# The dilation's first counts and first fixed point in turns with layer 0's last ending

## The chip, the cores and the metric

The kernel runs on one core of one Trainium2 chip. The metric is the device time of one execution in microseconds (us). The engines are named as the profile names them: PE (TensorE; PEld are its weight loads), DVE (VectorE), ACT (ScalarE), POOL (GpSimd), SP (SyncE, which here only issues DMAs). Each engine executes its own queue in order; engines wait for each other through semaphores. [...]

## What is computed

A graph of 1024 nodes with 128 features in each of 16 batches goes through four layers, each added to the running `x` and normed. Two of them matter here, cut to their core:

```python
# layer 0: attention over the adjacency, gate, then x + y, layernorm -> x1
h = x @ W_w.T + W_b
e = einsum('bjl,bkl->bjk', h @ A, h); e = e + swapaxes(e, 1, 2)
att = softmax(where(adj > 0, e, -9e15), axis=1) * adj
h_prime = relu(einsum('bij,bjk->bik', att, h))
coeff = sigmoid(concat([x, h_prime]) @ gate_w.T + gate_b)
y = coeff * x + (1 - coeff) * h_prime

# layer 1: first a sequential dilation of each adjacency, node by node
def step(carry, n):
    row = carry[n]
    num = sum(row)
    sf = where(num > 10, (num + 1) // 2, 1)
    rm = row & (cumsum(row) % sf == 0)      # which neighbours are removed
    keep = ~where(valid, rm, False)
    carry[n] = row & keep;  carry[:, n] = carry[:, n] & keep
# then three graph convolutions over x1 and the dilated adjacency
```

Layers 2 and 3 (a gated attention and a graph convolution) follow and are not touched.

## The kernel before

The batches are b = 0 to 15, NT = 8 tiles of 128 nodes each. The adjacencies of all batches stay in SBUF as 8-bit tiles `Y[b]` (`carry` in the profile), half of them on the left side of SBUF and half on the right.

**Layer 0** (L886 to L1033) runs three streams in rounds (`in_rounds`, L815; a stream yields the number of rounds it pauses). `before(b)` (L923) loads the rows of the adjacency (`an`), turns them to 8 bits, checks their symmetry and prepares the operands `xT`, `G`, `hn`. `attention(b)` (L968) computes scores in PSUM (`wide_matmul`, L724), takes minimum and mask on VectorE (L984), the exponential on ScalarE (L986), and weighs into `acc` (L974). `after(b)` (L999) ends a batch: `hpT` from `acc` (L1002), the gate by small matmuls (L775, L780) and a tanh (L1008), the mix on VectorE (L1014, L1016, L1017), the norm (`normed`, L787: statistics L794 and L796, power on GpSimd L745, `ln_nb` L799, eight activations on ScalarE L801), and the store of `x1_d` (L1020). While batch b is weighed, batch b - 1 ends and batch b + 1 begins. For batch 15 there is no next batch: L1033 runs `after(15)` by itself.

**The dilation** (L1043 to L1202) takes 16 steps: for each tile k of 128 nodes, two groups g of GB = 8 batches. `prepare` (L1057) counts the neighbours for four batches at a time: `uY` (L1072), 32 matmuls into `s0` (L1078), ranks `sk` (L1080), totals `l1` (L1081), `past` (L1084). `fixed_point` (L1089) finds the removals inside the tile in six evaluations, each a comparison `mid` on VectorE (L1106), eight small matmuls `pd` (L1109) and `ti` (L1113), and derives the bounds `negc`, `posc`, `wid` (L1116 to L1139). `removal` (L1142) applies them to one batch: matmuls `s` (L1151, L1153), two activations `q` (L1154), `keep` (L1157), the row update (L1158), the products `pc` (L1161 to L1165) and the write-back (L1166). In the loop (L1198) the fixed point of step i takes turns with the eight removals of step i - 1, which also prepare a later step. The first four `prepare` groups stand ahead of this loop (L1183), and the first round of the loop has the fixed point of step 0 alone. Between them are a flag (L1187, L1188) and `dinv` (L1190 to L1196).

**Layer 1** (L1267 on) starts with batches 8 to 15, whose adjacency needs no load. `first` (L1401) takes the degree product (L1290), copies it (`row`, L1406), sends it through a small DMA (`d`, L1408), and from there come `nodeg`, the reciprocal and the store of `rdeg` (L1409 to L1413). `split` makes `hi` (L1281) and `lo` (L1282) for the adjacency product (L1315); `widened` (L1302, L1304) casts the adjacency. `Step` (L1324) loads its small weights (`Wr`, `Wx`, `b`, `gcol`, `becol`; L703, L693, L698), and `take_norm` (L1341) begins with their sum `ws` (L1345).

**What sets the order.** The functions record instructions in the order of their yields. A scheduler then fixes each engine's queue, so an instruction may stand elsewhere than the source suggests. Pools place tiles in SBUF and PSUM as stacks, from the left or from the right side; a tile waits for the last readers and writers of tiles that lay in the same place before (`reuse_waits="tile"`: tile by tile).

Of the kernel before, what the change touches and what calls it, by code (L numbers as in the profile page):

```python
# [22 lines left out]
P = 128  # L23
# [616 lines left out]
def fast_kernel(ctx: ExitStack, tc: tile.TileContext, t: dict, out: bass.AP, flag: bass.AP):  # L640
# [245 lines left out]
    with ExitStack() as ph:  # L886

        early = ph.enter_context(tc.tile_pool(name="l0_early", bufs=1, reuse_waits="tile"))
        wts = ph.enter_context(tc.tile_pool(name="l0_w", bufs=1, reuse_waits="tile"))
        ps_w = ph.enter_context(tc.tile_pool(name="l0_pw", bufs=2, space=PSUM, reuse_waits="tile"))  # L890
        ps_a = ph.enter_context(tc.tile_pool(name="l0_pa", bufs=1, space=PSUM, reuse_waits="tile"))
        ps_h = ph.enter_context(tc.tile_pool(name="l0_ph", bufs=2, space=PSUM, reuse_waits="tile"))

        with tc.tile_pool(name="l0_raw", bufs=1) as raw:
            W0 = matrix(raw, t["L0_gnn_W_w"], "l0W")
            W0T = transposed(wts, ps_h, W0, "l0WT", "h")
            As0 = symmetric(raw, ps_h, matrix(raw, t["L0_gnn_A"], "l0A"), "l0As", "h")
            AW = raw.tile([P, P], F32, name="l0AW")
            p = ps_h.tile([P, P], F32, name="wtr", tag="h")
            nc.tensor.matmul(p, As0, W0, start=True, stop=True)  # L900
            nc.vector.tensor_copy(AW, p)
            M0 = wts.tile([P, P], F32, name="l0M")
            p = ps_h.tile([P, P], F32, name="wtr", tag="h")
            nc.tensor.matmul(p, W0, AW, start=True, stop=True)
            nc.vector.tensor_copy(M0, p)
            nu = wts.tile([P, 1], F32, name="l0nu")
            p = ps_h.tile([P, 1], F32, name="wtr", tag="h")
            nc.tensor.matmul(p, AW, column(raw, t["L0_gnn_W_b"], "l0b"), start=True, stop=True)
            nc.vector.tensor_scalar(nu, p, -1.0, None, op0=OP.mult)
        work = ph.enter_context(tc.tile_pool(name="l0_work", bufs=1, reuse_waits="tile"))  # L910
        small = ph.enter_context(tc.tile_pool(name="l0_small", bufs=2, reuse_waits="tile"))
        b0 = row_bcast(wts, t["L0_gnn_W_b"], P, "l0brow")
        gw = wts.tile([P, 2, 32], F32, name="l0gw")
        nc.vector.memset(gw, 0.0)
        with nc.allow_non_contiguous_dma(reason="a vector of 256"):
            nc.sync.dma_start(gw[:, :, 0], t["L0_gnn_gate_w"].rearrange("o (h d) -> d (o h)", d=P))
        gb = row_bcast(wts, t["L0_gnn_gate_b"], 1, "l0gb")
        gbh = wts.tile([P, 1], F32, name="l0gbh")
        nc.vector.tensor_scalar(gbh, gb, 0.5, None, op0=OP.mult)
        nbig = wts.tile([P, 1], F32, name="l0nbig")  # L920
        nc.vector.memset(nbig, BIG)

        def before(s, b):  # L923

            s.xn = work.tile([P, NT, P], F32, name="xn", bufs=3)
            nc.sync.dma_start(s.xn, nat(t["x"][b]))
            yield 1
            for it in range(NT):
                c = b * NT + it
                an = early.tile([P, N], F32, name="an", bufs=3)  # L930
                nc.sync.dma_start(an, t["adj"][b][it * P:(it + 1) * P, :])
                nc.scalar.activation(Y[b][:, it, :], an, AF.Copy, accum_out=deg[:, c:c + 1], saturate=False)  # L932

                chk = early.tile([P, N], FP8, name="chk")
                done = (it + 1) * P
                if done < N:
                    nc.vector.scalar_tensor_tensor(chk[:, done:], an[:, done:], 0.0, an[:, done:], op0=OP.is_gt,
                                                   op1=OP.not_equal, accum_out=other[:, b, it:it + 1], saturate=False)
                for h in range(it // 4 + 1):
                    js = range(4 * h, min(4 * h + 4, it + 1))  # L940
                    k = slice(js[0] * P, (js[-1] + 1) * P)
                    pt = ps_h.tile([P, 512], F32, name="pt", tag="h")
                    for i, jt in enumerate(js):
                        nc.tensor.matmul(pt[:, i * P:(i + 1) * P], Y[b][:, jt, it * P:done], identb, start=True, stop=True)
                    nc.vector.scalar_tensor_tensor(chk[:, k], pt[:, :k.stop - k.start], 0.0, an[:, k], op0=OP.is_gt,
                                                   op1=OP.not_equal, accum_out=other[:, b, 7 + it + 4 * h:8 + it + 4 * h],
                                                   saturate=False)
                if it == 2:
                    s.xT = work.tile([P, N], F32, name="xT", bufs=2)
                    for p, c, _ in turned(ps_h, s.xn):  # L950
                        nc.scalar.copy(s.xT[:, c], p)
                elif it == 4:
                    s.G = work.tile([P, N], F32, name="G", bufs=2)
                    for p, c in products(ps_h, (M0, s.xT)):
                        nc.scalar.activation(s.G[:, c], p, AF.Identity, scale=-1.0, bias=nu)
                    pz = gates(ps_h, early.tile([P, N], FP8, name="chk").bitcast(F32), (gw[:, 0, :], s.xT))
                    s.gx = small.tile([P, NT], F32, name="gx")
                    nc.vector.tensor_copy(s.gx.rearrange("p (q t) -> p q t", t=2), pz[:, :, :, 0])
                elif it == 5:
                    s.hn = work.tile([P, N], F32, name="hn")  # L960
                    for p, c, blocks in halves(ps_h):
                        for i, k in enumerate(blocks):
                            nc.tensor.matmul(p[:, i * P:(i + 1) * P], s.xT[:, k * P:(k + 1) * P], W0T, start=True, stop=True)
                        nc.vector.tensor_add(tiles3(s.hn[:, c]), tiles3(p), b0[:, None, :].to_broadcast([P, 4, P]))
                yield 2
            nc.gpsimd.dma_start(adj8_d[b], Y[b].bitcast(F32))

        def attention(s, b):  # L968
            s.acc = ps_a.tile([P, N], F32, name="acc")

            def weigh(jt, hs, em):
                for h in range(H2):
                    c = slice(h * 512, (h + 1) * 512)
                    nc.tensor.matmul(s.acc[:, c], hs, em[:, c], start=(jt == 0), stop=(jt == NT - 1))  # L974

            for jt in range(NT):
                js = slice(jt * P, (jt + 1) * P)
                c = b * NT + jt
                mn = mx0[:, c:c + 1]
                msk = work.tile([P, N], BF16, name="msk", bufs=2)  # L980
                nc.scalar.activation(msk, Y[b][:, jt, :], AF.Identity, scale=-BIG, bias=nbig)  # L981
                e = wide_matmul(ps_w, s.G[:, js], s.xT)
                em = work.tile([P, N], F32, name="em", bufs=2)
                nc.vector.tensor_tensor_reduce(em, e, msk, 1.0, 3.0e38, op0=OP.add, op1=OP.min, accum_out=mn)  # L984
                sm = small.tile([P, 1], F32, name="sm")
                nc.scalar.activation(em, em, AF.Exp, scale=-1.0, bias=mn, accum_out=sm)  # L986
                rs = small.tile([P, 1], F32, name="rs")
                nc.vector.reciprocal(rs, sm)
                hs = small.tile([P, P], F32, name="hs")
                nc.vector.tensor_scalar(hs, s.hn[:, js], rs, None, op0=OP.mult)  # L990
                yield
                if jt:
                    weigh(*late)
                late = jt, hs, em
                yield
            weigh(*late)
            yield

        def after(s, b):  # L999

            hpT = work.tile([P, N], F32, name="hpT")
            nc.scalar.activation(hpT, s.acc, AF.Relu)  # L1002
            yield 3
            pz = gates(ps_h, work.tile([P, NT, P], F32, name="r").rearrange("p t d -> p (t d)")[:, :N // 4], (gw[:, 1, :], hpT))
# [10 lines left out]
            for p, c, k in turned(ps_h, hpT):  # L1015
                nc.vector.tensor_mul(r[:, k, :], tiles3(p), half_rows(co[:, k]))  # L1016
# [8 lines left out]
        for b in range(B):  # L1025
            streams = []
            if b < B - 1:
                streams.append(before(state[b + 1], b + 1))
# [4 lines left out]
        in_rounds([after(state[B - 1], B - 1)])  # L1033

# [803 lines left out]
```

## Time and profile before

| | us |
|---|---|
| median of three runs | 2781.0 |
| lowest, highest | 2775.41, 2783.75 |
| profiled execution: time | 2779.18 |
| profiled execution: span of the instructions | 2777.5 |
| last weighing of layer 0 ends, about | 629.2 |
| layer 0's last activations L801 | 640.92 to 644.1 |
| store of batch 15's rows, from issue | 644.41, 3.9 to landing |
| first fixed point, first `mid` to the last one's end | 651.81 to 664.0 |
| first `q` of the removals | 666.77 |
| last write-back of the dilation, L1166 | 1017.09 to 1018.2 |

The profile records one execution. Its page gives the busy time of each engine over the span and in 40 slices (of 69.4 us here). Its trace answers questions about a stretch of time: a timeline of instructions (start, length, engine, line, operation, output from inputs; in brackets the engine's idle time just before and the instruction that ended it), the chain of waits (followed back from the end of the stretch, at each step to what released it; "issue" is time in which nothing is shown that the engine waited for), and the busy time of each engine in chosen windows, with the granted TensorE clock as a share of full speed. Runs of like instructions are merged (x8). Tile names come without their numbers: `l` is `l1`, `s` in L1078 is `s0`, `x_d` is `x1_d`, `carry` is `Y`.

### The profile page before, as it was taken

How to read it: one execution, taken by the hardware profiler on the slowest of the kernel's cores; microseconds unless marked ns; L12 is line 12 of the kernel's file. 1: busy time of each engine (PE TensorE's matmuls, PEld its weight loads, DVE VectorE, ACT ScalarE, POOL GpSimd, SP SyncE). 2: the span in 40 equal slices, each digit the busy share in tenths (PEclk: the TensorE clock that was granted, in tenths of full speed). 3: DMA queues.
4: the chain of work that ended last, by engine and by line, in shares of the span. 5: the costliest groups of instructions: out<-in, count | busy, mean ns of one | idle time of the engine just before them, and what ended most of it. 6: DMA issues, size and time to landing. Idle time of an engine off the chain costs nothing.

```text
span 2777.5 us, 41717 instructions
## 1 busy us (share of the span) xinstructions
PE 2586.3 (93%) x14808; PEld 1670.4 (60%) x14808; DVE 2131.3 (77%) x5905; ACT 1991.0 (72%) x3316; POOL 334.0 (12%) x287
## 2 busy tenths in 40 slices
PE   7999999995899879998999998999999999999985
PEld 3545444443666658877788894455555555555554
DVE  5888777876999967776788775777778777777865
ACT  6888888974888776666655445877777777777754
POOL 0000000030000002211122141011111111111100
PEclk9999999997999989999999998999999999999998
DMA  5555545520000052233467572111111111121000
GB/s 186 164 162 172 177 161 166 175 89 12 2 2 2 2 219 92 97 117 123 155 235 249 174 267 84 60 62 61 61 61 61 61 61 61 66 68 72 27 20 25
DMA packets 120810, 285.37 MB, mean 103 GB/s; under 512 B 12304, under 2 KB 65424, under 8 KB 113424
## 3 DMA queue, kind: packets, MB, share of 16 engines
q1 hardware_dynamic: 101280, 203.33, 22.3%
q0 software_dynamic: 19312, 79.28, 7.4%
q8 instruction: 119, 1.95, 0.3%
q14 instruction: 99, 0.81, 0.1%
HBM read 202.72 MB, written 79.82 MB: 102 GB/s over the span
## 4 chain that ended last, share of the span: by engine, by line
PE 40%; DVE 19%; ACT 9%; issue 9%; POOL 4%; DMA 3%; POOLq 0%; DVEq 0%; ACTq 0%; SPq 0%
PE pmm L724 6%; PE ph L1605 6%; PE acc L1315 5%; PE acc L1660 5%; PE ph L766 3%; PE ph L759 3%; ACT xn L801 3%; PE acc L974 2%; PE ph L1441 2%; POOL rn L745 2%; DVE em L1673 2%; DVE mid L1106 2%; PE ph L1592 2%; DVE ln_st L794 1%; PE s L1153 1%
## 5 line engine op out<-in xcount | busy, mean ns | idle before, releaser
L745 POOL TENSOR_TENSOR ln_rstd<-ln_rstd,mhalf 128x8 f32<-128x8 f32 (+1 forms) x68 | 121.6, 1788 | 1361.7 <-DVE ln_rstd L742 938.0
L724 PE MATMUL pmm<-xT,G 128*128 128x512 f32 x512 | 261.8, 604 | 0.0
L974 PE MATMUL acc<-em,hs 128*128 128x512 f32 x512 | 260.1, 607 | 1.3 <-DVE hs L990 1.1
L1315 PE MATMUL acc<-a,lo 128*128 128x512 f32 x768 | 240.0, 397 | 17.9 <-DVE lo L1282 17.9
L1660 PE MATMUL acc<-em,hs 128*128 128x512 f32 x512 | 248.6, 601 | 8.1 <-DVE hs L1684 7.8
L724 PE MATMUL pmm<-G,hT 128*128 128x512 f32 x512 | 245.0, 593 | 0.0
L1315 PE MATMUL acc<-a,hi 128*128 128x512 f32 x768 | 240.6, 398 | 3.0 <-ACT hi L1281 2.8
L801 ACT ACTIVATE xn<-xn,ln_nb,ln_rstd 128x128 f32<-128x128 f32 x512 | 205.0, 485 | 48.7 <-DVE ln_nb L799 48.7
L1668 ACT ACTIVATE msk<-A,nbig 128x1024 bf16<-128x1024 fp8e4 x128 | 147.1, 1150 | 73.7 <-DVE mx L1673 48.8
L986 ACT ACTIVATE em<-em,mx 128x1024 f32<-128x1024 f32 x128 | 146.8, 1147 | 59.6 <-DVE mx L984 59.2
L1315 PEld LDWEIGHTS acc<-a,lo 128*128 128x128 f32 x768 | 144.0, 190 | 54.6 <-DVE lo L1282 25.0
L984 DVE CUSTOM_DVE_ANT_0 em<-pmm,msk 128x1024 f32<-128x1024 f32 x128 | 156.3, 1221 | 23.2 <-PE pmm L724 22.4
L1673 DVE CUSTOM_DVE_ANT_0 em<-pmm,msk 128x1024 f32<-128x1024 f32 x128 | 156.3, 1221 | 11.6 <-PE pmm L724 11.3
L1315 PEld LDWEIGHTS acc<-a,hi 128*128 128x128 f32 x768 | 143.4, 190 | 33.1 <-ACT hi L1281 3.7
L1166 ACT ACTIVATE carry<-pc,negone 128x1024 fp8e4<-128x1024 f32 x128 | 141.0, 1115 | 24.4 <-PE pc L1165 19.9
L1605 PE MATMUL ph<-A,zhi 128*128 128x512 f32 x512 | 151.8, 438 | 1.5 <-ACT zhi L1595 1.3
L932 ACT ACTIVATE carry<-an 128x1024 fp8e4<-128x1024 f32 x128 | 134.7, 1052 | 25.9 <-DMA an<-in_adj 25.3
L1677 ACT ACTIVATE em<-em,nmx 128x1024 f32<-128x1024 f32 x128 | 146.2, 1142 | 8.1 <-DVE nmx L1675 7.8
L1660 PEld LDWEIGHTS acc<-em,hs 128*128 128x128 f32 x512 | 90.8, 191 | 92.7 <-issue 69.9
L981 ACT ACTIVATE msk<-carry,l0nbig 128x1024 bf16<-128x1024 fp8e4 x128 | 145.9, 1140 | 0.0
L1304 ACT CAST a<-carry 128x1024 fp32r<-128x1024 fp8e4 x96 | 99.5, 1050 | 50.4 <-PE acc L1315 50.3
L1304 ACT CAST a<-A 128x1024 fp32r<-128x1024 fp8e4 x96 | 99.2, 1050 | 50.3 <-PE acc L1315 50.3
(319 smaller groups left out, 6236.5 us busy)
## 6 DMA issues: line engine op xcount, KB each, us to landing
an<-in_adj SPq DMA_DIRECT2D x128, 512.0 KB, 3.7
adj_d<-carry POOLq DMA_DIRECT2D x16, 1024.0 KB, 4.2
A<-dil_d SPq DMA_DIRECT2D x16, 1024.0 KB, 5.5
rdeg<-rdeg_d SPq DMA_DIRECT2D x32, 512.0 KB, 3.8
A<-adj_d SPq DMA_DIRECT2D x16, 1024.0 KB, 4.8
ag_d<-ag POOLq DMA_DIRECT2D x24, 512.0 KB, 5.2
ag<-ag_d SPq DMA_DIRECT2D x24, 512.0 KB, 5.4
xn<-in_x SPq DMA_DIRECT2D x16, 512.0 KB, 4.3
```

The lines of the kernel that those rows point to most:

```text
L724: nc.tensor.matmul(p[:, h * 512:(h + 1) * 512], lhsT, rhs[:, h * 512:(h + 1) * 512], start=True, stop=True)
L745: nc.gpsimd.tensor_tensor(r, r, mhalf[:, :n], op=OP.pow)
L801: nc.scalar.activation(r[:, k.start + i, :], r[:, k.start + i, :], AF.Identity, scale=rstd[:, i:i + 1], bias=nb[:, i:i + 1])
L974: nc.tensor.matmul(s.acc[:, c], hs, em[:, c], start=(jt == 0), stop=(jt == NT - 1))
L984: nc.vector.tensor_tensor_reduce(em, e, msk, 1.0, 3.0e38, op0=OP.add, op1=OP.min, accum_out=mn)
L986: nc.scalar.activation(em, em, AF.Exp, scale=-1.0, bias=mn, accum_out=sm)
L1304: nc.scalar.copy(a, A[:, 2 * i:2 * i + 2, c])
L1315: nc.tensor.matmul(acc, part[:, jt, :], pieces[h * NT // 2 + i][:, j, :], start=(jt == 0 and p == 0), stop=(jt == NT - 1 and p == 1))
L1605: nc.tensor.matmul(p, part[:, jt, :], A[:, jt, c], start=(jt == 0 and i == 0), stop=(jt == NT - 1 and i == 1))
L1660: nc.tensor.matmul(s.acc[:, c], hs, ex[:, c], start=(jt == 0), stop=(jt == NT - 1))
L1668: nc.scalar.activation(msk, s.A8[:, jt, :], AF.Identity, scale=BIG, bias=nbig, accum_out=zs)
L1673: nc.vector.tensor_tensor_reduce(em, e, msk, 1.0, 0.0, op0=OP.add, op1=OP.max, accum_out=mx)
```

## The change

Layer 0's pools are no longer closed at its end as one. Two stacks of contexts take them: `scores` holds the adjacency's rows (`early`) and the scores' PSUM (`ps_w`), both now on the right side; `ending` holds the rest, on the left. `scores` is closed after the last round of layer 0, and the dilation's pools (SBUF and PSUM, except `ps_c`) are opened on the right side, where those lay. A new stream chains the four `prepare` groups and the fixed point of step 0, and runs in rounds with `after(15)`. Then `ending` is closed, `ps_c` is opened on the left, and the loop starts at step 1. The dilation's pool `small` is renamed `tiny`, since `after` still uses layer 0's `small`. The body of layer 0 is moved out of its `with` block unchanged.

```diff
+    ending, scores = ExitStack(), ExitStack()
+
+    early = scores.enter_context(tc.tile_pool(name="l0_early", bufs=1, side="right", reuse_waits="tile"))
+    wts = ending.enter_context(tc.tile_pool(name="l0_w", bufs=1, reuse_waits="tile"))
+    ps_w = scores.enter_context(tc.tile_pool(name="l0_pw", bufs=2, space=PSUM, side="right", reuse_waits="tile"))
+    ps_a = ending.enter_context(tc.tile_pool(name="l0_pa", bufs=1, space=PSUM, reuse_waits="tile"))
+    ps_h = ending.enter_context(tc.tile_pool(name="l0_ph", bufs=2, space=PSUM, reuse_waits="tile"))
...
+    work = ending.enter_context(tc.tile_pool(name="l0_work", bufs=1, reuse_waits="tile"))
+    small = ending.enter_context(tc.tile_pool(name="l0_small", bufs=2, reuse_waits="tile"))
...
-        in_rounds([after(state[B - 1], B - 1)])
...
+        in_rounds(streams)
+    scores.close()
+
     with ExitStack() as ph:
...
-        sb = ph.enter_context(tc.tile_pool(name="dl_sb", bufs=2, reuse_waits="tile"))
-        small = ph.enter_context(tc.tile_pool(name="dl_small", bufs=3, reuse_waits="tile"))
-        ps_b = ph.enter_context(tc.tile_pool(name="dl_pb", bufs=1, space=PSUM, reuse_waits="tile"))
-        ps_d = ph.enter_context(tc.tile_pool(name="dl_pd", bufs=1, space=PSUM, reuse_waits="tile"))
-        ps_s = ph.enter_context(tc.tile_pool(name="dl_ps", bufs=2, space=PSUM, reuse_waits="tile"))
-        ps_c = ph.enter_context(tc.tile_pool(name="dl_pc", bufs=2, space=PSUM, reuse_waits="tile"))
+        sb = ph.enter_context(tc.tile_pool(name="dl_sb", bufs=2, side="right", reuse_waits="tile"))
+        tiny = ph.enter_context(tc.tile_pool(name="dl_small", bufs=3, side="right", reuse_waits="tile"))
+        ps_b = ph.enter_context(tc.tile_pool(name="dl_pb", bufs=1, space=PSUM, side="right", reuse_waits="tile"))
+        ps_d = ph.enter_context(tc.tile_pool(name="dl_pd", bufs=1, space=PSUM, side="right", reuse_waits="tile"))
+        ps_s = ph.enter_context(tc.tile_pool(name="dl_ps", bufs=2, space=PSUM, side="right", reuse_waits="tile"))
...
-        for s in steps[:G2]:
-            for _ in prepare(*s):
-                pass
+        in_rounds([chain(*(prepare(*s) for s in steps[:G2]), fixed_point(*steps[0])), after(state[B - 1], B - 1)])
+        ending.close()
+        ps_c = ph.enter_context(tc.tile_pool(name="dl_pc", bufs=2, space=PSUM, reuse_waits="tile"))
...
-        for i in range(len(steps) + 1):
+        for i in range(1, len(steps) + 1):
             streams = [fixed_point(*steps[i])] if i < len(steps) else []
-            if i:
-                streams.append(removals(steps[i - 1], steps[i - 1 + G2] if i - 1 + G2 < len(steps) else None))
+            streams.append(removals(steps[i - 1], steps[i - 1 + G2] if i - 1 + G2 < len(steps) else None))
             take_turns(streams)
```

## The prediction, made before the result was known

> **What bounds the kernel now.** I read the page's totals first, then the chain of waits from 600 to 700 us, then the engines' timeline there and at the start of layer 1. The totals:
>
> ```profile
> span 2777.5 us, 41717 instructions
> PE 2586.3 (93%) x14808; PEld 1670.4 (60%) x14808; DVE 2131.3 (77%) x5905; ACT 1991.0 (72%) x3316; POOL 334.0 (12%) x287
> ```
>
> TensorE is busy 93% of the span, but slice 10 of 40 (625 to 694 us) has it at half, and this is where the change acts. The chain of waits there (start, length, what):
>
> ```profile
> 627.27 1.97 PE acc L974 x4
> 629.26 1.03 ACT hpT L1002
> ...
> 639.03 1.66 POOL ln_rstd L745
> 640.69 3.71 issue
> 644.41 3.86 DMA x_d<-xn
> 648.53 0.20 DVE uY L1072
> 648.85 1.32 PE s L1078 x32
> ...
> 662.84 1.24 DVE mid L1106
> 664.12 0.37 PE pd L1109 x8
> 664.50 1.20 PE s L1153 x4
> 665.70 1.08 PE s L1151 x4
> 666.78 0.69 ACT q L1154
> ```
>
> The last weighing ends at 629.2. Then one thread runs alone: batch 15's gate and norm, the store of its rows, the dilation's first counts, six evaluations of the first fixed point. Only at 666.78 does the first removal begin. The timeline (start, length, engine, then in brackets the idle time before and who ended it) says why the counts came so late:
>
> ```profile
> 640.92 3.19 ACT L801 ACTIVATE xn<-xn,ln_nb,ln_rstd 128x128 f32<-128x128 f32 x8 [8.47 <-DVE ln_nb L799]
> 648.37 0.16 DVE L1081 SCALAR_TENSOR_TENSOR l<-s,off 128x4 f32<-128x4 f32 x1 [6.47 <-DMA x_d<-xn]
> 1026.73 0.27 DVE L1409 TENSOR_REDUCE nodeg<-d 8x1 f32<-8x128 f16 x1 [8.72 <-DMA d<-row]
> 1029.24 1.22 PE L1315 MATMUL acc<-a,lo 128*128 128x512 f32 x2 [5.56 <-DVE lo L1282]
> ```
>
> VectorE's first `l1` stood 6.47 us for a store: its small buffer lies where batch 15's `xn` lay. The last two rows are layer 1's start, which the change touches too. The stage tables (length, busy times, granted clock) close the reading:
>
> ```profile
> 629.30:648.50 19.20, 1.99 (x18) 1.28 (x19) 7.73 (x30) 4.86 (x11) 2.58 (x2) 0.68 0.09 27
> 648.50:664.00 15.50, 5.83 (x136) 5.17 (x135) 12.58 (x37) 0.00 (x0) 0.00 (x0) 0.50 0.02 6
> ```
>
> No engine is full in the first stretch; in the second VectorE is busy 12.58 of 15.5 us, TensorE 5.83.
>
> **The change part by part.** No arithmetic goes; it is order and place. I lined up both programs' instructions: up to VectorE's last reduction of the scores (624.10) they differ by two `uY` (0.49 us), placed at 601 us where VectorE idles 0.76 us: nothing. After the dilation's second removal step the orders are equal up to layer 1's start.
>
> *The walk.* I take VectorE's new order, instruction by instruction, with the lengths of before, starting a wait where its producer ends.
> - The first `sk` (0.61) now stands ahead of the last reciprocal, and needs counts that end at 626.55. The last weighing starts 0.6 us later than at 627.27 and ends at 629.85; `hpT` ends at 630.9.
> - TensorE's second group of counts follows that weighing: 629.65 to 630.85. Its `sk` ends at 631.55. From there to the first `mid` it takes 1.0 us (650.80 to 651.81 before): `mid` at 632.6.
> - Before, from first to last `mid` (651.81 to 663.98) it took 12.2 us with the last counts between. Now batch 15's ending stands between: VectorE instructions of 0.24 (gates), 1.14, 2 x 0.65, 1.2, 1.55 (eight statistics), 0.58, 0.2, together 6.2 us. If all of it fell into the waits for `pd` the fixed point would end at 644.8, if none, at 651.0. Following the queue (of each 2.1 us evaluation VectorE works 1.4), 4.1 us stay on the path, since the wide ones (1.14, 1.2) are longer than any gap: 632.6 + 12.2 + 4.1 = 648.9. Before it was 663.98: **15.1 us earlier**.
> - New waits. `ln_nb` stands behind the last `mid` and waits for GpSimd's power: 2.0 us from `ln_rstd` on, as 638.71 to 640.72 before. Queued behind it are `negc`, `posc` and the second fixed point's first `mid`: about 1.1 us of stall. ScalarE has the eight `xn` (3.19) ahead of the first `q`. So 649.0 + 2.0 + 0.2 + 3.2 = 654.4 for the first `q`, against 666.77: **12.4 us earlier**. The second fixed point is 13.5 us ahead; the removals hold the step, so I take 12.4.
>
> *Batch 15's store* lands later, at about 654.4 + 0.3 + 3.9 = 658.6 instead of 648.3. GpSimd's next work is a store at 977.55; layer 1 reads these rows eighth, beyond 1100 us: covered by hundreds of us. But SP's queue meets it. Layer 1's left pools now lie on layer 0's memory, not the dilation's, so its small weights load during the dilation; `b` waits for this store, and behind it stand `gcol`, `becol`, the second `Wr` and `Wx` (rows of 0.45 to 0.69 between issues: the last at 661.3). The scheduler moved the addition that reads them, L1345, from layer 1 into VectorE's queue in the first removal step, with five removals queued behind it. By my walk VectorE gets there at 665.4. A load of this kind landed after 2.1 us (least) to 9.1 (most, among 3 MB of others): 663.4 to 670.4. With SP's queue otherwise empty I take 2.1 to 4.4 and a cost of 0; upper end 5 us.
>
> *dinv and the flags* (L1187 to L1196): moved a few us, 0.8 us of VectorE, with its copy in the stall between the first two counts (628 to 631): 0.
>
> *Layer 1's start.* The degree product's accumulator no longer lies on the removals' last bank, and stands ahead of the last removal's products. The four `row` copies move ahead of two casts of 1 us (18.09 to 20.08 after 1000 before): the path row, store, `d`, `lo` starts 1.9 us earlier. The first loads of `n`, issued at 1015.10 behind VectorE's last `keep`, now follow the loads at 1005.9, so `d<-row` meets less traffic: 5.0 us before, 2.0 in the median of its kind. Lower end 0, upper 1.9 + 3.0 = 4.9; I take **3.0**, as `lo` also needs `hi`, which ends at 1022.4 either way.
>
> [...] The first removals run at a granted clock of 0.5: four matmuls of 128x512 took 1.20 and 1.08 us, later 0.71. [...]
>
> Sum: 12.4 + 3.0 = 15.4. The profiled execution took 2779.2 (span 2777.5 and 1.7 around it), which makes 2763.8; the median of the three runs shown, 2781.0, is 1.8 above it, so **2765.6**. Measured times spread 2775 to 2784, so 0.3%, 8.3 us, is about what this kernel's measurement can tell from no change.
>
> **The rivals.**
> - *The lead is partly given back in the first removal step* (chance 0.2). Three `mid` of the second fixed point now stand ahead of the first `keep`, and products come in bunches ahead of ScalarE's write-backs. A step of before took about 22.1 us (16 steps from 664 to 1018) and needs 19.44 of VectorE in its first 22, so an order that leaves VectorE waiting is not caught up. If 5 us go here and layer 1's start gives 1: 12.4 - 5 + 1 = 8.4, 2772.6. For it: the new order was made on modelled costs. Against it: the same instructions, and later steps regain nothing but lose nothing.
> - *More than I count* (0.2): the clock stays up (2.6) and layer 1's start gives its 4.9: 19.9, 2761.1. Against it is the row above.
> - *The order hides it all* (0.04): within 3 us of before, 2779. VectorE was idle 11.5 of 19.2 us, and no other engine fills that gap, which speaks against it.
> - *Slower than before* (0.03), at L1345: VectorE stops until `Wx` lands. The price is landing minus 665.4. Up to 665.4 it costs nothing, at 670.4 five us; it undoes the gain only from 681 on, and to lose 0.3% it must be 689, a landing 28 us after issue. Nothing of the kind is in the trace, whose slowest such load took 9.1.
> - The likeliest, as summed: 0.53.
>
> The change does move what it says: the new VectorE order has the counts and all six evaluations among batch 15's instructions.
>
> **How the numbers follow.** The likeliest case holds 2761 to 2770 with the spread of a median. The given-back case and the large case lie on both sides, at 2772.6 and 2761.1, and their own spread takes the range to 2756 and 2776. Below 2772.7 lie the likeliest, the large case and about half of the given-back one: faster 0.85; same 0.12; slower 0.03.
>
> **What would show it.** Right: no wait of `l1` for the store; last `mid` of the first fixed point near 649; first `q` near 654.4, directly after ScalarE's eight `xn`; the dilation's last write-back 12 to 13 us earlier than 1018; layer 1's `row` right after it; granted clock near 0.5 at the first removals. Wrong: first `q` after 658 (more of the ending on the path than 4.1 us); a wait at L1345; a removal step of more than 24 us; a layer 1 start that begins earlier and reaches its first `lo` product no sooner.

## The result, and the profile after

Ten runs of the changed kernel have a median of 2767.23 us (2762.59 to 2776.23); the kernel before, on the same chip, 2781.04. The ratio is 0.995, with a 95% interval of 0.9936 to 0.9964: about 13.8 us less, 10 to 18 by the interval. The profiled execution took 2765.43, against 2779.18 before; both spans differ by 13.8 as well. Forecast were 2765.6 for the median and 2763.8 for the profiled execution.

The page's totals of the changed kernel: the same work in a shorter span.

```profile
span 2763.7 us, 41707 instructions
PE 2584.2 (94%) x14808; PEld 1667.1 (60%) x14808; DVE 2129.5 (77%) x5905; ACT 1987.7 (72%) x3316; POOL 331.9 (12%) x287
```

The chain of waits from 600 to 700 us, changed kernel (start, length, what):

```profile
627.89 1.96 PE acc L974 x4
629.85 0.92 PE s L1069 x32
...
632.40 1.23 DVE mid L1097
...
648.80 1.66 POOL ln_rstd L745
...
651.12 1.14 DVE mid L1097
...
654.78 1.09 PE s L1144 x4
```

The store is gone from it, and the first `mid` follows the last weighing by 2.5 us instead of 22.6. The timeline's rows that answer to those of before:

```profile
627.34 0.14 DVE L1072 SCALAR_TENSOR_TENSOR l<-s,off 128x4 f32<-128x4 f32 x1
650.49 0.17 DVE L799 SCALAR_TENSOR_TENSOR ln_nb<-ln_mv,ln_rstd 128x8 f32<-128x8 f32 x1 [0.91 <-POOL ln_rstd L745]
650.69 3.19 ACT L801 ACTIVATE xn<-xn,ln_nb,ln_rstd 128x128 f32<-128x128 f32 x8 [15.99 <-DVE ln_nb L799]
653.78 0.67 ACT L1145 ACTIVATE q<-s,negc 128x512 f16<-128x512 f32 x1
665.30 0.29 DVE L1335 TENSOR_TENSOR ws<-Wr,Wx 128x128 f32<-128x128 f32 x1
1012.90 0.27 DVE L1399 TENSOR_REDUCE nodeg<-d 8x1 f32<-8x128 f16 x1 [6.83 <-DMA d<-row]
1015.41 1.22 PE L1305 MATMUL acc<-a,lo 128*128 128x512 f32 x2 [2.85 <-DVE lo L1272]
```

The first `l1` no longer waits. `ln_nb` waits 0.91 us for GpSimd, and the first `q` starts as the eight `xn` end: 653.78 instead of 666.77, 13.0 us earlier. `ws` stands there without a wait. The stage table (length, busy times of PE, PEld, DVE, ACT and POOL with their counts, then granted clock, DMA share and GB/s), cut at the new boundaries:

```profile
629.90:648.50 18.60, 6.69 (x154) 5.25 (x149) 17.35 (x57) 1.68 (x3) 0.00 (x0) 0.76 0.03 8
648.50:654.00 5.50, 3.04 (x24) 1.58 (x24) 4.28 (x22) 3.31 (x9) 1.65 (x1) 0.50 0.00 0
654.00:676.00 22.00, 19.06 (x223) 13.25 (x224) 17.38 (x48) 17.23 (x24) 0.93 (x1) 0.86 0.16 37
```

Two thin stretches have become one in which VectorE is busy 17.35 of 18.6 us. So far this is the forecast walk. Whether the turns in the change's name make the gain, its place in memory, or both, one trace can't say.

### The profile page after: what moved, and what is told of

Its sections match the earlier page's. It is cut to its first block, busy times and chain, and to the rows that moved or that the text cites. A ratio compares the mean times of both kernels' runs of the same rounds, so it can differ in the third digit from the quotient of the medians.

```text
span 2763.7 us, 41707 instructions
## 1 busy us (share of the span) xinstructions
PE 2584.2 (94%) x14808; PEld 1667.1 (60%) x14808; DVE 2129.5 (77%) x5905; ACT 1987.7 (72%) x3316; POOL 331.9 (12%) x287
## 4 chain that ended last, share of the span: by engine, by line
PE 54%; DVE 19%; ACT 10%; issue 8%; DMA 4%; POOL 4%; SPq 0%; POOLq 0%; DVEq 0%; ACTq 0%
PE pmm L724 11%; PE acc L974 8%; PE ph L1595 6%; PE acc L1305 6%; PE acc L1650 5%; PE ph L766 4%; PE ph L759 3%; ACT xn L801 3%; POOL rn L745 2%; DVE em L1663 2%; PE ph L1431 2%; DMA xn<-x_d 2%; DVE ln_st L794 2%; PE ph L1582 1%; DVE mid L1097 1%
## 5 line engine op out<-in xcount | busy, mean ns | idle before, releaser
L1305 PEld LDWEIGHTS acc<-a,lo 128*128 128x128 f32 x768 | 144.0, 190 | 52.0 <-DVE lo L1272 22.5
L1663 DVE CUSTOM_DVE_ANT_0 em<-pmm,msk 128x1024 f32<-128x1024 f32 x128 | 155.9, 1218 | 11.4 <-PE pmm L724 11.1
L724 PEld LDWEIGHTS pmm<-G,hT 128*128 128x128 f32 x512 | 90.2, 190 | 74.6 <-issue 71.2
```

What stands on the lines that cost most here:

```text
L724: nc.tensor.matmul(p[:, h * 512:(h + 1) * 512], lhsT, rhs[:, h * 512:(h + 1) * 512], start=True, stop=True)
L1305: nc.tensor.matmul(acc, part[:, jt, :], pieces[h * NT // 2 + i][:, j, :], start=(jt == 0 and p == 0), stop=(jt == NT - 1 and p == 1))
L1663: nc.vector.tensor_tensor_reduce(em, e, msk, 1.0, 0.0, op0=OP.add, op1=OP.max, accum_out=mx)
```

## The experiments

Up to batch 14's `hpT` the kernels of this table do the same work, and yet its start lies between 597.6 and 599.4 us in their traces. So I count, in each trace, from the start of batch 15's `hpT` (629.26 before, 629.89 changed). The turns don't move it; the SBUF place does, by 0.5 us (31.3 to 31.4 us behind batch 14's instead of 30.8), and the table leaves that out. The last column is the stretch from the dilation's last write-back to the last start of an `ag` (1374.8 before), the front half of layer 1. All in us:

| trace | first `q` | first `keep` of the third removal step | last write-back | from there to `row` | to `lo` | to the last `ag` |
|---|---|---|---|---|---|---|
| before | 37.5 | 82.6 | 387.8 | 2.88 | 10.95 | 357.7 |
| changed | 23.9 | 71.2 | 375.2 | 1.01 | 9.09 | 355.4 |
| changed, second trace | 23.9 | 70.6 | 376.4 | 1.01 | 9.24 | 355.8 |
| SBUF place alone | 26.0 | 71.1 | 376.3 | 2.89 | 5.35 | 352.6 |
| both places, old order | 26.0 | 71.0 | 377.1 | 1.01 | 9.53 | 355.7 |
| PSUM ends alone | 37.5 | 83.4 | 387.8 | 1.01 | 8.84 | 355.7 |
| changed, PSUM mirrored | 23.9 | 71.0 | 376.3 | 2.89 | 5.35 | 353.5 |
| ending's tail moved on | 22.5 | 68.5 | 372.4 | 1.01 | 9.33 | 356.6 |
| tail moved, PSUM mirrored | 22.5 | 67.8 | 371.9 | 2.89 | 5.36 | 352.7 |

A bank, below, is the place of one `s` tile (128x512 f32) in PSUM. My theory at this point: the store's wait, the turns and layer 1's start each bring their part. The rivals are in the expectations.

**SBUF place alone.** Edit, against the changed kernel:

```diff
+    in_rounds([after(state[B - 1], B - 1)])
+    ending.close()
...
-        in_rounds([chain(*(prepare(*s) for s in steps[:G2]), fixed_point(*steps[0])), after(state[B - 1], B - 1)])
-        ending.close()
...
+        take_turns([chain(*(prepare(*s) for s in steps[:G2]), fixed_point(*steps[0]))])
```

The ending stands ahead of the dilation's pools, and all PSUM pools lie at the left end, `ps_w` and the dilation's `dl_pb`, `dl_pd` and `dl_ps` over the same banks, as before.

> The kernel before with one thing of the change: the dilation's SBUF pools lie at the right, where the adjacency's rows were, so that its counts need not wait for the store of batch 15's x1. The text of the program keeps the old order (the ending whole, then the counts, then the first fixed point), and the PSUM pools lie as before. My theory (the gain is the store's wait, then the turns, then some 2 to 4 us at layer 1's start that hang on where PSUM lies): the counts run at 627 as in the changed kernel, the first mid at about 632.4, the second only behind the ending's VectorE work at about 643, the first q at about 657 against 666.8 before and 653.8 after; layer 1's start gains nothing of its own; about 2771 to 2774 us. Rival A (the turns are what counts, the place alone does little): the first mid stays near 650, above 2777 us. Rival B (place alone gives all of it, the order in the text nothing): first q at 654, within 1 us of the changed kernel, 2767.

Measured: 2763.43 us against 2783.38, ratio 0.9938 (0.9921 to 0.9955). The timeline of this kernel:

```profile
631.46 1.22 DVE L1099 TENSOR_TENSOR mid<-sk,thr 128x1024 fp8e4<-128x1024 f16 x1
642.57 1.22 DVE L1099 TENSOR_TENSOR mid<-sk,thr 128x1024 fp8e4<-128x1024 f16 x1
654.89 0.69 ACT L1147 ACTIVATE q<-s,negc 128x512 f16<-128x512 f32 x1 [9.37 <-PE s L1144]
1010.55 1.22 DVE L1273 TENSOR_TENSOR lo<-n,hi 128x1024 fp32r<-128x1024 f32 x1 [4.43 <-ACT hi L1272]
1013.53 0.27 DVE L1400 TENSOR_REDUCE nodeg<-d 8x1 f32<-8x128 f16 x1 [1.75 <-DMA d<-row]
```

The first `mid` comes at 631.46 though the text has it behind the whole ending: once the memory is free, the scheduler itself takes the counts ahead. The second stands behind the ending's VectorE work, as I had it. The `q` is 11.5 us earlier than before on the common origin, 2.1 later than with the turns. My theory of where things stand was right, of the sum wrong: 2771 to 2774 were expected, and the interval ends at 2770.9 (0.9955 of 2783.38). Two things were missed. The last two rows show one: here `lo` stands ahead of the reduction that waits for `d`, while in the changed kernel it stands behind. The other shows in the table's third column, and the next run bears it out.

**Both places, old order.** The changed kernel with only this edit:

```diff
-        in_rounds([chain(*(prepare(*s) for s in steps[:G2]), fixed_point(*steps[0])), after(state[B - 1], B - 1)])
+        in_rounds([after(state[B - 1], B - 1)])
+        take_turns([chain(*(prepare(*s) for s in steps[:G2]), fixed_point(*steps[0]))])
```

> The changed kernel with its pools where it has them, SBUF and PSUM, but in the old order: the ending whole, then the counts and the first fixed point. My theory: the same first q as with the SBUF place alone (about 657), so 3 us behind the changed kernel, and with the PSUM place layer 1's start gains as in the changed kernel (first product of lo 14 us or more earlier than before less those 3, its first write-back L1441 another 1.9): about 2770 us. Rival B (place gives all, order nothing): 2767. Rival C (layer 1's gain does not come from PSUM's place): the same time as with the SBUF place alone.

Measured: 2768.33, ratio 0.9951 (0.9935 to 0.9966), the changed kernel's figure. The interval, 2765 to 2774, holds my 2770 and the rival's 2767 alike, so the traces have to decide. The turns' 2.1 us at the first `q` are there, and by the third removal step they are gone: 71.2 and 70.6 with turns, 71.0 without. Second removal step, from its first `keep` to the third step's, with turns and then, in the second fence, in the old order:

```profile
677.80:701.10 23.30, 19.13 (x255) 13.60 (x253) 21.92 (x65) 19.18 (x27) 0.00 (x0) 1.00 0.01 2
```

```profile
680.70:701.70 21.00, 18.46 (x251) 13.16 (x249) 20.12 (x59) 18.13 (x25) 0.00 (x0) 1.00 0.01 2
```

With turns VectorE has 65 instructions and 21.92 us in that step, in the old order 59 and 20.12. In the step ahead of it the counts are the other way round, 47 with turns and 57 in the old order: what the turns push out of the first step falls into the second. From the third on all orders are alike. Rival B was right in its total, not in its mechanism: order does move the first `q`, but the second step takes it back.

**PSUM ends alone.** The kernel before, with this edit (and the same for `dl_pd` and `dl_ps`):

```diff
-        ps_b = ph.enter_context(tc.tile_pool(name="dl_pb", bufs=1, space=PSUM, reuse_waits="tile"))
+        ps_b = ph.enter_context(tc.tile_pool(name="dl_pb", bufs=1, space=PSUM, side="right", reuse_waits="tile"))
```

> The kernel before with only the PSUM pools of the dilation's counts, degrees and scores at the right end, so that the write-back's PSUM lies at the left end; SBUF and order as before. My theory: the first q stays at 667 or comes some tenths of a us later; at layer 1's start the row copies no longer meet the write-backs' banks and lie 1.9 us earlier, the first lo product with them, and the write-backs of layer 1 follow 2 to 4 us earlier: 2777 to 2779 us. Rival C (layer 1's gain comes with the lead and not with PSUM's place): 2781, no change.

Measured: 2779.97 against 2783.38, ratio 0.999 (0.9983 to 0.9996), so 1 to 5 us less. `row` follows the last write-back after 1.01 us instead of 2.88, `lo` after 8.84 instead of 10.95, and the last `ag` is 2.0 us nearer. As expected; rival C is out, for a kernel whose SBUF is as before.

**The changed kernel again, and with PSUM mirrored.** The mirrored one exchanges the sides of all PSUM pools of layer 0 and the dilation (`ps_w`, `dl_pb`, `dl_pd`, `dl_ps` left; `ps_a`, `ps_h`, `ps_c` right); of its lines one pair:

```diff
-        ps_c = ph.enter_context(tc.tile_pool(name="dl_pc", bufs=2, space=PSUM, reuse_waits="tile"))
+        ps_c = ph.enter_context(tc.tile_pool(name="dl_pc", bufs=2, space=PSUM, side="right", reuse_waits="tile"))
```

> The changed kernel once more, beside the next three on one chip. Theory: the 2 us of its lead that its first trace lost within layer 2 (15.8 us ahead at the end of layer 1, 13.8 at the end) are run-to-run drift: 2766 to 2769 us, and in its second trace the stretch from the end of layer 1 to the end of the kernel differs from the first one's by 1 us or more. Rival: they belong to the change: that stretch stays within 0.3 us of the first trace's.

> The changed kernel with the two ends of PSUM exchanged, so that the dilation's write-back lies at the right end, as before, under the banks that layer 1's degree and adjacency products take; turns and SBUF as changed. The prediction's theory (the row copies at layer 1's start wait for the last write-back's banks): the row copies fall back by 1.9 us and the start of layer 1 by 2 to 4: 2769 to 2771 us. Theory after the run with the SBUF place alone: with the write-back at the right the engines' order at layer 1's start is another one (lo on VectorE ahead of the reduction that waits for d, the second batch's degree products on TensorE in the gap), lo comes some 5.4 us behind the last write-back instead of 9.1, and layer 1 is 1 to 3 us ahead of the changed kernel's: 2764 to 2766 us. First q 653.8 by both.

Measured against one 2778.47: 2767.49, ratio 0.9957 (0.994 to 0.9973), and mirrored 2762.72, ratio 0.9937 (0.992 to 0.9954). In the two traces of the changed kernel the stretch from layer 1's last squares to the end takes 1105.5 and 1102.4 us, so the 2 us that seemed lost in layer 2 are drift (before, at 1103.5, lies between). The two intervals overlap, so the times alone don't set the mirrored kernel apart; it came out below both expectations. The mirrored trace at layer 1's start:

```profile
1008.99 1.48 ACT L1396 CAST row<-acc 1x256 f16<-1x256 f32 x4
1010.76 0.52 POOL L1398 DMA_DIRECT2D d<-row  x1 [21.73 <-ACT row L1396]
1011.45 1.23 DVE L1272 TENSOR_TENSOR lo<-n,hi 128x1024 fp32r<-128x1024 f32 x1 [4.43 <-ACT hi L1271]
1013.55 0.27 DVE L1399 TENSOR_REDUCE nodeg<-d 8x1 f32<-8x128 f16 x1 [0.87 <-DMA d<-row]
```

`row` is late again, by 1.9 us, as the prediction's theory has it; but `lo` is 2.8 us earlier than the changed kernel's 1014.21, and the front half of layer 1 takes 353.5 us instead of 355.4. So the prediction had the wrong path there. `hi` ends 5.3 us behind the last write-back in every trace, that of before included:

```profile
1021.37 1.04 ACT L1281 CAST hi<-n 128x1024 fp32r<-128x1024 f32 x1
```

`lo` could have started there; what differs is its place in VectorE's queue, ahead of `nodeg` or behind `nodeg`'s wait for `d`.

With the new SBUF place an early `row` buys little: `d<-row`, issued at 1007.89, let its reader start at 1012.90 in the changed kernel; issued 2.9 us later here, at 1013.55. In all six traces with an early `row` it took 4.7 to 5.4 us, in the five with a late one and the new SBUF place 2.7 to 3.8; before, it took 5.0. What moves between is the loads, in the mirrored kernel and then in the changed one:

```profile
1008.00:1010.00 2.00, 0.00 (x0) 0.00 (x0) 0.00 (x0) 1.98 (x5) 0.00 (x0) 1.00 1.15 366
1010.00:1012.00 2.00, 0.53 (x1) 0.50 (x2) 0.55 (x1) 1.96 (x5) 0.52 (x1) 0.75 0.67 268
1012.00:1014.00 2.00, 2.00 (x11) 0.80 (x9) 1.10 (x4) 1.46 (x3) 0.00 (x0) 0.50 0.02 8
```

```profile
1008.00:1010.00 2.00, 0.00 (x0) 0.00 (x0) 0.00 (x0) 2.00 (x3) 0.41 (x1) 0.56 1.06 402
1010.00:1012.00 2.00, 1.51 (x4) 1.16 (x4) 0.00 (x0) 1.98 (x4) 0.00 (x0) 0.50 0.31 124
1012.00:1013.00 1.00, 0.56 (x2) 0.00 (x0) 0.10 (x1) 0.48 (x1) 0.00 (x0) 0.50 0.02 8
```

In both the small transfer lands once 370 to 400 GB/s of loads have ebbed, around 1012, though it was issued 2.9 us apart. That the loads hold it up is read from this, not tried by itself.

**The ending's tail moved on.** `after(15)` in two parts, its norm and store in the first removal step's turns (`ps_a` and `ps_h` are closed ahead of `ps_c`, the SBUF behind that step):

```diff
-        in_rounds([chain(...), after(state[B - 1], B - 1)])
+        last = after(state[B - 1], B - 1)
+        in_rounds([chain(...), islice(last, 3)])
...
+            if i == 1:
+                streams.append(last)
             take_turns(streams)
```

> The changed kernel with the last part of batch 15's ending (its norm and its store) moved on into the turns of the first removal step, so that ScalarE's eight xn (3.19 us) no longer all lie ahead of the first q. My theory (xn ahead of the first q is on the path): the first q comes 1.3 to 2.6 us earlier than 653.8, the step's end less than that, since ScalarE is 17.2 of 22 us busy there: 2765 to 2766.5 us. Rival D (TensorE at its low clock sets the first removals, xn is hidden): within 0.5 us of the changed kernel. Rival E: the xn between the q's delay the second and third removal by their 3.2 us, and the time is the changed kernel's or up to 1 us more.

Measured: 2764.43, ratio 0.9932 (0.9916 to 0.9947). The timeline of this kernel:

```profile
650.70 1.66 ACT L801 ACTIVATE xn<-xn,ln_nb,ln_rstd 128x128 f32<-128x128 f32 x4 [16.00 <-DVE ln_nb L799]
652.36 0.69 ACT L1145 ACTIVATE q<-s,negc 128x512 f16<-128x512 f32 x1
```

Four of the eight `xn` moved behind the first two `q`, and these come 1.4 us earlier. Unlike the turns' gain this one lasts: against the changed kernel's two traces 2.7 and 2.1 us at the third removal step, 2.8 and 4.0 at the last write-back. The expectation had less left at the step's end than at the `q`, which was wrong. So `xn` ahead of `q` is on the path, and by the traces rivals D and E fall; the times alone, 0.9932 against 0.995 and 0.9957 with intervals that overlap, would not decide it.

**Step 0 a round earlier.** Step 0 needs batches 0 to 7 alone. Its counts and fixed point go beside batch 15's attention, and batch 15's ending into the first removal step's turns; the adjacency's rows close a round earlier, counts (`s0`) and degrees (`pd`) take layer 0's PSUM tag `h`, two banks in turn, and `ps_c` the scores' place. The second kernel is its twin with PSUM mirrored:

```diff
+        else:
+            rows.close()
...
+            streams.append(chain(prepare(*steps[0]), fixed_point(*steps[0]), prepare(*steps[1])))
         streams.append(attention(state[b], b))
...
-                s0 = ps_b.tile([P, QB, P], F32, name="s0")
+            s0 = ps_h.tile([P, QB, P], F32, name="s0", tag="h")
```

> Step 0's counts and fixed point moved one round further ahead, beside batch 15's attention (they need batches 0 to 7 alone), in the SBUF of the adjacency's rows, which close one round earlier, and in the PSUM that layer 0's ending uses; batch 15's ending then runs in turns with the first removal step, and the write-back takes the scores' PSUM. Theory (the removals' start is what holds the path from 629.9 to 653.8, where TensorE is busy 9.7 of 24 us): TensorE's 6 to 7 us of counts come on top of the attention's round, in which it is busy throughout, the first q follows the last weighing at 633 to 637 instead of 653.8, ScalarE and VectorE carry the ending beside the removals, and 8 to 13 us are gained on the changed kernel: 2754 to 2759 us. Rival (VectorE's queue: each of the six rounds of the fixed point holds up the attention's minimum behind a wait for TensorE): the last weighing is late by 10 us or more and the gain is 0 to 5 us: 2762 to 2767 us.

> The same with the two ends of PSUM exchanged: the write-back at the left end, clear of the banks of layer 1's degree products. Theory of the prediction (PSUM's place at layer 1's start is worth 2 to 4 us): 2 to 4 us less than its twin. Theory after the run with the SBUF place alone (the place decides only which of two orders layer 1's start takes: row copies first and lo behind the wait for d, or lo first): row copies 1.0 us behind the last write-back and lo 9 us behind it, the twin 2.9 and 5.4; this one 0 to 3 us longer than its twin.

Measured: 2762.18, ratio 0.9937 (0.9918 to 0.9956), and the twin 2765.57, ratio 0.9949 (0.993 to 0.9968). The twin bears out the second theory by its trace: `row` 1.01 and `lo` 9.25 us behind the last write-back instead of 2.89 and 5.35, and a front half of layer 1 that takes 1.8 us more. The rival's mechanism of the first run is there too: `hpT` starts at 640.1, 10.2 us late. Still the first `q` stands at 642.1, 11.7 us ahead of the changed kernel. But the lead melts: 8.3 us at the third removal step, 6.8 two steps later, 0.7 at the ninth, 0.2 at the last write-back. Neither side had that. The total waits from 743 to 827 us (waiting instruction, who ended it: sum, times, longest), this kernel first, then the changed one:

```profile
ACT carry L1138 <- PE pc L1137: 14.1, 17, 3.0
PEld L1081 <- DVE mid L1078: 6.3, 15, 1.8
PE s L1123 <- ACT q L1126: 5.4, 12, 0.9
```

```profile
PEld L1100 <- DVE mid L1097: 7.5, 19, 1.0
ACT q L1145 <- PE pc L1156: 4.8, 4, 1.3
ACT carry L1157 <- PE pc L1156: 3.9, 4, 1.0
```

ScalarE's write-backs wait 14.1 us for TensorE instead of 3.9, and the longest wait for a `mid` is 1.8 us instead of 1.0. My suspicion fell on `s0` and `pd`, which now take turns in the same two banks. So, at the end of the first removal step:

```diff
+        if i == 1:
+            ending.close()
+            count = ph.enter_context(tc.tile_pool(name="dl_pb", bufs=1, space=PSUM, reuse_waits="tile")), "s0"
+            degrees = ph.enter_context(tc.tile_pool(name="dl_pd", bufs=1, space=PSUM, reuse_waits="tile")), "pd"
```

> The kernel with step 0's counts and fixed point beside batch 15's attention, now with a PSUM bank each for the counts and the degrees from the second step on; in the run before, both took turns in the two banks of layer 0's ending to the end of the dilation. Theory (that sharing is what gave the lead back: 8.3 us ahead of the changed kernel at the third step, then 0.8 us less in every step, and nothing left at the last write-back): the steps take the changed kernel's time again, 7 to 9 us of lead remain at the last write-back (996 to 998), 2753 to 2757 us. Rival (another order of the engines behind the moved ending gives it back): the last write-back stays at 1003 to 1006, 2760 to 2763 us.

Measured: 2756.83 against 2777.03, ratio 0.9925 (0.991 to 0.9941), 20 us less than before (16 to 25 by the interval, which overlaps that of the run without these banks). The lead is 8.8 us at the third step and 8.6 at the last write-back. Same waits, same window:

```profile
PEld L1081 <- DVE mid L1078: 7.9, 19, 1.0
ACT q L1126 <- PE pc L1137: 4.8, 4, 1.3
ACT carry L1138 <- PE pc L1137: 3.9, 4, 1.0
```

They are the changed kernel's again, and the steps from the third on are as long as the changed kernel's: the sharing is by far the likeliest cause. The edit also moves `dl_ps` to the right end and closes `ending` behind the first removal step instead of behind the dilation; neither was run by itself.

**Tail and mirror together.**

> Two edits that helped, together: batch 15's norm and store in the turns of the first removal step, and the two ends of PSUM exchanged. If they add up (2.9 us at the last write-back, some 2.5 us more at layer 1's start by the order with lo first): 5 us less than the changed kernel, 2760 to 2763 us, the last write-back at 1002 to 1003 and the first lo 5.4 us behind it. Rival: layer 1's order flips back or the lead is lost on the way: 2764 to 2766 us.

Measured: 2760.3, ratio 0.9933 (0.9919 to 0.9947). The two add up in the table: 371.9 at the last write-back, then 5.36 to `lo`. The ratio is the tail's alone (0.9932), so the times show no gain of the mirror beside it.

## Why the prediction held, step by step

- *The walk to the first `q`: right.* First `mid` 632.40 (632.6), the fixed point's last `mid` ends at 648.5 (648.9), stall of `ln_nb` 0.91 us (1.1), first `q` 653.78 (654.4). It rests on reading the new VectorE queue with old durations, and on two findings in it: 4.1 of the ending's 6.2 us stay on the path, and `xn` stands ahead of `q`. The second was tested by the moved tail; the 4.1 is borne out by the end it leads to, 648.5, and by nothing else.
- *L1345: right.* Reached at 665.30 (665.4), no wait; its `Wx`, issued at 661.14 (661.3), took 2.2 us to land.
- *The clock: right.* It was 0.50 when the first removals ran: from 639.59 to 660.07 us in the changed kernel, from 636.02 to 673.57 before. No run shows the 2.6 us that the large rival has for a clock that stays up. In the changed kernel's trace four matmuls of 128x512 into `s` took 1.23 to 1.27 us from 648.89 to 659.3, in that of before 1.22 to 1.27 from 664.45 to 671.1; with the clock at 1.00 again, 0.70 to 0.71. TensorE's longest gap in the new stretch was 3.40 us, and the clock had fallen early in it, as told below.
- *"12.4 carries through to layer 1": a little too much.* On each trace's own clock the lead is 13.0 and 13.6 us at the first `q` in the changed kernel's two traces, 10.7 and 11.9 at the third removal step, 12.0 and 11.4 at the last write-back. I had the instruction orders as equal from the third step on, which is so; the second step, 23.3 us instead of 21.0 in both, is where 2.3 us go. This is what the rival with the lead given back said, in size about 2 us, not 5. That the first trace has 12.0 again at the end is luck, as I read the next rows.
- *The luck of the clock.* The thirteenth removal step, before and then changed, from first `keep` to first `keep`:

```profile
923.05:950.65 27.60, 23.37 (x328) 18.67 (x326) 24.95 (x73) 20.62 (x26) 0.00 (x0) 0.93 0.00 1
912.28:938.69 26.41, 22.28 (x327) 17.54 (x325) 24.94 (x73) 20.48 (x26) 0.00 (x0) 0.96 0.00 1
```

It is the same work, but TensorE is busy 1.1 us longer before, at the lower granted clock, and the step is 1.2 us longer: before, 3.69 us of it stand at 0.50 (923.05 to 926.14 and the last 0.60), in the changed kernel 2.14 (936.55 to 938.69). That the clock makes the difference is my reading of these two traces.

- *Layer 1's start, 3.0: the term was mis-sized, since its two parts don't add.* The 1.9 us of `row` came (2.88 to 1.01). The traffic's share did not come on top: `d<-row` took 5.0 us, as before. It does exist where `row` is late (2.7 to 3.8 us), but the reader of `d` starts 7.4 to 8.5 us behind the last write-back in every other trace and 9.6 before, whichever of the two parts a kernel has. (The prediction's 2.0 for "the median of its kind" was misread too: the page of before has 2.4 for `d<-row`, which makes the upper end of the term 4.5.) From the last write-back to the last `ag` the changed kernel saved 2.3 and 1.9 us in two traces, the PSUM ends alone 2.0. And I missed what the SBUF place did: with it, and with the write-back's banks as before, the scheduler puts `lo` first, in all five traces of that kind, and 3.2 to 5.1 us are saved. Exchanging the ends gave about half of it away. `n` is loaded from 995.35 instead of 1015.10, which may be why the scheduler chooses so; that isn't shown.
- *The sum.* 15.4 forecast, 13.8 measured. The terms as measured on the common origin: 12.6 and 11.5 us at the dilation's end in two traces, 2.3 and 1.9 at layer 1's start, less 0.6 and 0.1 by which layer 0's end came later than before, make 14.3 and 13.3; the two spans are 13.8 and 12.9 shorter. The chances were added a little high: the likeliest, the large and half of the given-back case make 0.83, not 0.85.
- *What the change's name says* was not what acted. The SBUF place alone brings 11.5 of 13.6 us at the first `q` and, from the third step on, all. The prediction didn't need this split for its number, but an engineer who takes the change for proof that turns pay would be wrong here.

What stays open: whether the loads alone hold `d` up, and why the scheduler takes `lo` first in some of these programs.

## What to carry to other kernels

Where a scheduler orders the instructions, free the memory first, and look whether order written by hand adds anything: follow a gain past the point where it appears until orders are equal again. When stages overlap, give each accumulator that is on a loop's path its own bank; with two that shared two banks, ScalarE's write-backs waited 14.1 us for TensorE from 743 to 827 us instead of 3.9, and of a lead of 8.3 us 0.2 was left at the last write-back. And a place that removes one wait can change which instruction the scheduler puts first at the next stage, so test both ends.

## What the chip did that I had not expected

The clock fell 1.1 us into a gap of TensorE. In the changed kernel, from left to right length, busy times (TensorE first) and in the third column from the end the granted clock, in stretches of 3.41 us, the shortest time at half clock in this trace between 600 and 1040 us:

```profile
632.77:636.18 3.41, 2.89 (x59) 2.35 (x56) 3.41 (x12) 0.30 (x1) 0.00 (x0) 1.00 0.02 5
636.18:639.59 3.41, 0.35 (x8) 0.27 (x8) 3.41 (x11) 0.00 (x0) 0.00 (x0) 1.00 0.01 2
639.59:643.00 3.41, 0.37 (x8) 0.29 (x8) 3.34 (x9) 0.00 (x0) 0.00 (x0) 0.50 0.00 0
653.24:656.66 3.42, 2.25 (x16) 1.24 (x17) 2.88 (x5) 2.47 (x5) 0.93 (x1) 0.50 0.29 85
656.66:660.07 3.41, 3.41 (x23) 1.95 (x22) 1.95 (x5) 2.06 (x3) 0.00 (x0) 0.50 0.25 73
660.07:663.48 3.41, 3.23 (x59) 2.69 (x58) 2.68 (x6) 2.83 (x3) 0.00 (x0) 1.00 0.35 69
```

TensorE's last dense work ended at 636.05; then came eight degree products `pd` (0.35 us) at 638.10, and the next at 641.85. The trace has the fall at 639.59: 3.5 us behind the dense work, but only 1.1 us into the gap. The eight products in between did not keep it at 1.00. It came back at 660.07, 20.48 us later.

The figure 3.41 is read from the two traces. Between 600 and 1040 us that of before has five times at half clock: 37.55 us (636.02 to 673.57), three of 3.41 (from 922.73, 950.05 and 997.84) and 13.65 (from 1021.72). That of the changed kernel has five as well: 20.48 us (the one above), three of 3.41 (from 936.55, 960.45 and 984.35) and 10.24 (from 1008.23). Counted in times of 3.41 us they are 11, 1, 1, 1, 4 and 6, 1, 1, 1, 3. Why they are whole multiples, the traces don't show.

In the last 3.41 us ahead of the fall TensorE was busy 0.35 us here and 0.23 before. In the last 3.41 us ahead of the return it was busy throughout in both traces; in the 3.41 us before those, 2.25 us here and 2.86 before (from 666.75), and behind these the clock stayed at 0.50. What sets it, and how little work lets it fall, one fall and one return in each of two traces don't show.
